# One copy of an expert's first two products for each of four slot counts, chosen at run time by a jump on three engines

## The chip, the cores and the metric

The kernel runs on one core of a Trainium2 chip. The time is the device time of one execution in microseconds (us); lower is better. The core has TensorE (PE in the profile; its weight loads are PEld), VectorE (DVE), ScalarE (ACT), GpSimd (POOL) and SyncE (SP). Each engine works through its own queue of instructions in order and waits on semaphores for the others. DMAs are issued from SP's queue (SPq) and, for the scattered writes, from POOL's.

## The reference: one decoder layer that ends in a mixture of experts

Everything is float32 with 8 x 512 tokens of width 512. The layer is a Mamba block, a cross-attention and a mixture of experts (MoE), each followed by a residual and a LayerNorm. Only the experts matter here:

```python
cap = max(1, int(CAP_FACTOR * N * K / E))            # 640 slots for each of 32 experts
...
pos = (jnp.cumsum(oh, axis=0) * oh).sum(-1) - 1       # place of a token within its expert
keep = pos < cap
...
xe = xp[buf_tok].reshape(E, cap, DIM)                 # unused slots hold zeros
h = jax.nn.silu(jnp.einsum('ecd,edh->ech', xe, w1)) * jnp.einsum('ecd,edh->ech', xe, w3)
out = jnp.einsum('ech,ehd->ecd', h, w2) * buf_w.reshape(E, cap, 1)
y = jnp.zeros((N + 1, DIM), x.dtype).at[buf_tok].add(out.reshape(E * cap, DIM))[:N]
```

A token goes to 4 of 32 experts, so an expert gets 512 tokens on average; every expert has 640 slots, and the slots beyond its tokens are zero rows. With the inputs that the reference sets up, the gate sends these numbers of tokens to experts 0 to 31: 728 555 429 316 439 394 503 606 368 498 370 383 616 500 344 750 553 400 539 555 679 620 480 671 353 536 560 691 680 400 394 474. So 12 experts have at most 448 tokens, 5 have 449 to 512, 6 have 513 to 576 and 9 have more than 576.

## The kernel before: three stages, and the experts one after the other

`layers` (to about 3784 us in the profiled execution) computes the Mamba block, the attention, the gate and the shared expert, and scatters each token's row of 545 numbers (512 features, 32 weights, the token's number) to its slots in a DRAM buffer `xbuf`. `experts` then loops over the 32 experts, and `finish` reads the sums `based` and normalises them.

For each expert `e` the loop does this:

- `load(e + 1)`: SP issues the DMA of the next expert's 640 rows, `xe` (L1250), and then of its weights `w1`, `w3`, `w2` (L1253). The pools hold two of each. So `xe` of expert e+1 goes into the buffer of expert e-1, and must wait until everything that reads that buffer is done. The last readers are the scatters of e-1, which take the token numbers from it.
- `hidden(got, r, side)` for r = 0 and 1: the products of `xe` with `w1` and `w3` by Winograd's form of Strassen's scheme, seven products of quarter size in place of eight. The slots are the moving columns, two halves of 320 (`HALF`). `product` (L1314) is two float32 matmuls, which the trace shows as two records each; seven products for two weights and two r make 112 matmul records for each expert. ACT copies partial sums from PSUM (L1328) and applies SiLU (L1341), DVE adds and multiplies (L1335, L1339) into `hT`.
- `give(e, got, side)`: the product with `w2`, again seven quarter products, 256 columns wide, for the first 512 slots (56 records of `ps_o`), and a plain product `po` (L1416, 8 records) for the last 128 slots. ACT (L1387, L1417, L1444) and DVE (L1391) scale by the token's weight into five tiles `y`. Each is added to `based` by an indirect DMA from POOL (L1394, `put`), first the one of `po`, then the other four. They wait for each other, since all add to the same tensor.
- `side` is work for the next expert that is threaded in: `between` transposes `xe` of e+1 (`flip`: four PE transposes L1285 into one PSUM bank of the pool `e_pst`, one DVE copy L1286) and forms the sums of its slots (`sums_x`, L1293 to L1296) and of its weights (`sums_w` L1276, `sums_w2` L1308).

A scheduler fixes the order on each engine from the program's order, the dependencies and its own idea of times. In its order the transposes of expert e+1 are spread over `give(e)`: one group of four at its start, the other four groups between the products. On DVE the sums for the weights come in `give` and at its end, after the sums of `hT`.

Of the kernel before, what the change touches and what calls it, by code (L numbers as in the profile page):

```python
# [8 lines left out]
F32 = mybir.dt.float32  # L9
I32 = mybir.dt.int32  # L10
# [7 lines left out]
P = 128  # L18
# [21 lines left out]
E = 32  # L40
# [6 lines left out]
SLOTS = E * CAP  # L47
CJ = CAP // P
HALF = CAP // 2

ROW = D + E + 1

# [33 lines left out]
    return wait(roots)  # L86


def layers(ctx, tc, a, x1d, filld, based, xbuf):

# [572 lines left out]
    def locate(any_, pb, pn, st):  # L663
        for j in range(SC):
            nc.vector.tensor_tensor(taken[:, j + 1, :], taken[:, j, :], pn[:, j * E : (j + 1) * E], ALU.add)
        pos = new([E], "g_sc")
        nc.vector.tensor_tensor(
            pos, pb.rearrange("p (j e) -> p j e", j=SC), taken[:, 0:SC, :], ALU.add
        )
        nc.vector.tensor_copy(taken[:, 0, :], taken[:, SC, :])  # L670
        fits = new([E], "g_fits")
        nc.vector.tensor_scalar(fits, pos, float(CAP), None, ALU.is_lt)
        nc.vector.tensor_tensor(pos, pos, first, ALU.add)
        nc.vector.tensor_tensor(pos, pos, fits, ALU.mult)
# [542 lines left out]
    dry()  # L1217


def experts(ctx, tc, a, xbuf, based):  # L1220

# [40 lines left out]
    def B(x, j, k):  # L1262
        return x[:, 2 * j : 2 * j + 2, k * HALF : (k + 1) * HALF]

    def sums_w(got, n):

        w = got[n]
        s1, s2, s4 = (wp.tile([P, 2, FH], F32, tag=f"{n}s{i}", name="s", bufs=1 if n == "hT" else 2) for i in (1, 2, 4))
        got[n, "s"] = s1, s2, A(w, 1, 0), s4
        for o, x, y, op in (  # L1270
            (s1, A(w, 1, 0), A(w, 1, 1), ALU.add),
            (s2, s1, A(w, 0, 0), ALU.subtract),
            (A(w, 1, 0), A(w, 0, 0), A(w, 1, 0), ALU.subtract),
            (s4, A(w, 0, 1), s2, ALU.subtract),
        ):
            nc.vector.tensor_tensor(o, x, y, op)  # L1276
            yield

    def flip(got, j):

        if j == 0:
            got["xT"] = p2.tile([P, DC, CAP], F32, tag="xT", name="xT")
        ps = pst.tile([P, D], F32, tag="tr", name="ps_t")
        for dc in range(DC):
            nc.tensor.transpose(ps[:, dc * P : (dc + 1) * P], got["x"][:, j, dc * P : (dc + 1) * P], ident)  # L1285
        nc.vector.tensor_copy(got["xT"][:, :, j * P : (j + 1) * P], ps.rearrange("p (c t) -> p c t", c=DC))  # L1286

    def sums_x(got):

# [5 lines left out]
        nc.vector.tensor_tensor(B(x, 0, 1), B(x, 1, 1), B(x, 0, 1), ALU.subtract)  # L1295
        nc.vector.tensor_tensor(t4, B(x, 1, 0), t2, ALU.subtract)  # L1296

    def sums_w2(got):

        w = got["w2"]  # L1300
        got["t2"] = t1, t2, t3, t4 = [wp.tile([P, 2, FH], F32, tag=f"w2t{i}", name="t", bufs=1) for i in range(4)]
        for o, x, y in (
            (t1, BW(w, 0, 1), BW(w, 0, 0)),
            (t2, BW(w, 1, 1), t1),
            (t3, BW(w, 1, 1), BW(w, 0, 1)),
            (t4, BW(w, 1, 0), t2),
        ):
            nc.vector.tensor_tensor(o, x, y, ALU.subtract)  # L1308
            yield

    def product(ps, w, r, x, more=False):

        for n in range(2):
            nc.tensor.matmul(  # L1314
                ps, w[:, n, r * P : (r + 1) * P], x[:, n, :], start=not more and n == 0, stop=n == 1,
                skip_group_check=more,
            )

    def hidden(got, r, side):

        x, hT = got["xT"], got["hT"]
        t1, t2, t3, t4 = got["t"]
        ws = [(got[n], *got[n, "s"]) for n in ("w1", "w3")]
        both = range(2)

        def keep(ps, m, tag):
            v = p2.tile([P, HALF], F32, tag=f"{tag}{m}", name=tag)
            nc.scalar.copy(v, ps)  # L1328
            return v

        def use(m, i, k, ps, more=None):
            to = hT[:, 2 * i + r, k * HALF : (k + 1) * HALF]
            if more is not None:
                v = more if m else to
                nc.vector.tensor_tensor(v, ps, more, ALU.add)  # L1335
            else:
                v = ps
            if m:
                nc.vector.tensor_tensor(to, to, v, ALU.mult)  # L1339
            else:  # L1340
                nc.scalar.activation(to, v, AF.Silu)  # L1341

        p1, pu, p5 = [], [], []
        xs = [None, None]
        for m, (w, s1, s2, s3, s4) in enumerate(ws):
            xs[m] = psx.tile([P, HALF], F32, tag="h", name="ps_h")
            product(xs[m], A(w, 0, 0), r, B(x, 0, 0))
            p1.append(keep(xs[m], m, "p1"))
        for m, (w, s1, s2, s3, s4) in enumerate(ws):
            ps = psy.tile([P, HALF], F32, tag="h2", name="ps_h")  # L1350
            product(ps, A(w, 0, 1), r, B(x, 1, 0))
            use(m, 0, 0, ps, p1[m])
        next(side, None)
        for m, (w, s1, s2, s3, s4) in enumerate(ws):
            product(xs[m], s2, r, t2, more=True)
            pu.append(keep(xs[m], m, "pu"))
        next(side, None)
        ys = []
        for m, (w, s1, s2, s3, s4) in enumerate(ws):
            ys.append(psy.tile([P, HALF], F32, tag="h2", name="ps_h"))  # L1360
            product(ys[m], s1, r, t1)
            p5.append(keep(ys[m], m, "p5"))
        next(side, None)
        for m, (w, s1, s2, s3, s4) in enumerate(ws):
            product(xs[m], s3, r, t3, more=True)
            use(m, 1, 1, xs[m], p5[m])
        for m, (w, s1, s2, s3, s4) in enumerate(ws):
            product(ys[m], s4, r, B(x, 1, 1), more=True)
            use(m, 0, 1, ys[m], pu[m])
        next(side, None)  # L1370
        for m, (w, s1, s2, s3, s4) in enumerate(ws):
            product(xs[m], A(w, 1, 1), r, t4, more=True)
            use(m, 1, 0, xs[m])

    def give(e, got, side):

        xe, hT, w2 = got["x"], got["hT"], got["w2"]
        t1, t2, t3, t4 = got["t2"]
# [34 lines left out]
        j = CJ - 1  # L1413
        po = pso.tile([P, D], F32, tag="po", name="po")
        for ic in range(DC):
            nc.tensor.matmul(po, hT[:, ic, j * P : (j + 1) * P], w2[:, ic, :], start=(ic == 0), stop=(ic == DC - 1))  # L1416
        nc.scalar.activation(ys[j], po, AF.Identity, scale=weight(j))  # L1417
        put(j)
        next(side, None)
# [26 lines left out]

    def between(nxt):

        sums = sums_w(nxt, "w3")
        for j in range(CJ):  # L1450
            flip(nxt, j)
# [2 lines left out]
            next(sums, None)  # L1454
            yield

    nxt = load(0)
    for j in range(CJ):
        flip(nxt, j)
    sums_x(nxt)  # L1460
    for n in ("w1", "w3"):
        for _ in sums_w(nxt, n):
# [53 lines left out]

def program(tc, a, out):
    nc = tc.nc
    with tc.tile_pool(name="dram", bufs=1, space=DRAM) as dram:
# [4 lines left out]
        xbuf = dram.tile([SLOTS, ROW], F32, name="xbuf")  # L1524
        nc.scalar.preload_act_table_set(LN_EXP)

        with ExitStack() as ctx:
            layers(ctx, tc, a, x1d, filld, based, xbuf)
        with ExitStack() as ctx:
            experts(ctx, tc, a, xbuf, based)  # L1530
        with ExitStack() as ctx:
            finish(ctx, tc, based, out)

# [30 lines left out]
```

## Time and profile before

| | |
|---|---|
| time, median of 3 runs | 5404.11 us (5396.59 to 5407.47) |
| time of the profiled execution | 5406.28 us |
| its span, first to last instruction | 5404.6 us |
| experts' matmuls, first and last start | 3800.6 and 5333 us |
| one expert, start of its transposes to the next one's | 47.9 us |
| busy over the span | PE 86%, DVE 78%, ACT 48%, POOL 11% |

An engine's line in the profile gives start and duration in us, the source line, the output and inputs, and in brackets how long the engine stood idle before and what ended that. A matmul's duration overlaps the next one's start, so rates are taken from one group's start to the next one's. "Granted clock" (PEclk) is the share of full speed at which TensorE was let run.

### The profile page before, as it was taken

How to read it: one execution, taken by the hardware profiler on the slowest of the kernel's cores; microseconds unless marked ns; L12 is line 12 of the kernel's file. 1: busy time of each engine (PE TensorE's matmuls, PEld its weight loads, DVE VectorE, ACT ScalarE, POOL GpSimd, SP SyncE). 2: the span in 40 equal slices, each digit the busy share in tenths (PEclk: the TensorE clock that was granted, in tenths of full speed). 3: DMA queues.
4: the chain of work that ended last, by engine and by line, in shares of the span. 5: the costliest groups of instructions: out<-in, count | busy, mean ns of one | idle time of the engine just before them, and what ended most of it. 6: DMA issues, size and time to landing. Idle time of an engine off the chain costs nothing. (4 is left out here: it accounts for less than half of the span.)

```text
span 5404.6 us, 53991 instructions
## 1 busy us (share of the span) xinstructions
PE 4672.4 (86%) x17320; PEld 2476.6 (46%) x17320; DVE 4235.9 (78%) x5369; ACT 2593.6 (48%) x5726; POOL 570.3 (11%) x426
## 2 busy tenths in 40 slices
PE   6768889788888988988888888789999999999994
PEld 3324234234333423433333342333677777777773
DVE  7999899989989989898998998943566555665554
ACT  5566565565656556566565655523222222222223
POOL 1000002002000200200200020011111111111111
PEclk8879989999999999999999999899999999999997
DMA  8875346345444634634544463342344444544544
GB/s 236 266 224 146 87 96 208 81 114 176 114 104 117 197 77 109 189 98 107 174 125 100 117 200 78 91 146 66 103 128 127 123 117 118 127 127 121 129 115 144
DMA packets 486427, 719.03 MB, mean 133 GB/s; under 512 B 117137, under 2 KB 200625, under 8 KB 484096
## 3 DMA queue, kind: packets, MB, share of 16 engines
q1 hardware_dynamic: 450128, 627.16, 41.1%
q0 software_dynamic: 33280, 76.90, 7.5%
q10 hardware_dynamic: 2736, 11.54, 0.5%
q8 instruction: 137, 2.24, 0.2%
q14 instruction: 146, 1.20, 0.1%
HBM read 391.24 MB, written 165.05 MB: 103 GB/s over the span
## 5 line engine op out<-in xcount | busy, mean ns | idle before, releaser
L480 ACT ACTIVATE l_da<-rep,l_aneg 128x256 f32<-128x256 f32 x2048 | 895.0, 501 | 941.8 <-DVE h L501 877.0
L501 DVE TENSOR_TENSOR_SCAN h<-l_da,h 128x1028 f32<-128x1028 f32 x512 | 1166.0, 2292 | 20.3 <-ACT l_da L480 17.7
L494 DVE TENSOR_TENSOR h<-rep,bc 128x1024 f32<-128x1024 f32 x512 | 614.7, 1218 | 103.1 <-PE py L521 84.6
L510 DVE TENSOR_TENSOR h<-h,bc 128x1024 f32<-128x1024 f32 x512 | 619.5, 1217 | 2.1
L521 PE MATMUL py<-h,l_fold 128*32 128x512 f32 x2048 | 368.3, 644 | 113.4 <-DVE h L510 96.5
L813 PE MATMUL ps_s<-l_ka,l_qa 64*128 64x512 f32 x1024 | 325.6, 707 | 137.8 <-DVE mx L815 137.6
L1314 PE MATMUL ps_h<-xT,w 128*128 128x320 f32 x1536 | 435.8, 433 | 0.0
L1394 POOL DMA_INDIRECT based<-y,xe x160 | 255.5, 1597 | 1309.9 <-ACT y L1417 630.0
L1335 DVE TENSOR_TENSOR hT<-ps_h,p 128x320 f32<-128x320 f32 x128 | 62.9, 492 | 378.5 <-PE ps_h L1314 378.5
L815 DVE TENSOR_REDUCE mx<-ps_s 128x2 f32<-128x1024 f32 x256 | 310.2, 1217 | 58.5 <-PE ps_s L813 58.3
L1314 PEld LDWEIGHTS ps_h<-xT,w 128*128 128x128 f32 x1536 | 292.5, 191 | 118.3 <-issue 0.4
L855 PE MATMUL po<-eT,l_va 128*64 128x512 f32 x1024 | 301.5, 670 | 47.6 <-ACT eT L843 43.1
L839 PE MATMUL ps_t<-l_qa,l_ka 64*128 64x512 f32 x1024 | 308.4, 674 | 23.8 <-ACT eT L843 23.1
L843 ACT ACTIVATE eT<-ps_t 128x1024 f32<-128x1024 f32 x256 | 259.0, 1015 | 128.8 <-PE ps_t L839 128.5
L688 POOL DMA_INDIRECT xbuf<-x2t,dest x128 | 217.2, 1697 | 860.4 <-DVE dest L679 760.8
L1314 PE MATMUL ps_h<-t,s 128*128 128x320 f32 x1024 | 286.1, 432 | 0.0
L343 PE MATMUL ps_z<-xnT,wm 128*128 128x256 f32 x1024 | 238.0, 388 | 30.0 <-DVE o L561 24.3
L750 PE MATMUL ps_p<-x2T,wa 128*128 128x512 f32 x512 | 241.5, 626 | 18.1 <-ACT hT L944 10.4
L552 PE MATMUL po<-wm,zs 128*128 128x512 f32 x512 | 244.7, 632 | 13.8 <-DVE z L957 11.9
L343 PE MATMUL ps_x<-xnT,wm 128*128 128x256 f32 x1024 | 246.5, 393 | 4.5 <-ACT xnT L332 2.5
L343 PEld LDWEIGHTS ps_z<-xnT,wm 128*128 128x128 f32 x1024 | 194.6, 193 | 93.0 <-DVE o L561 37.5
L343 PEld LDWEIGHTS ps_x<-xnT,wm 128*128 128x128 f32 x1024 | 196.1, 195 | 80.5 <-issue 43.8
(232 smaller groups left out, 7170.4 us busy)
## 6 DMA issues: line engine op xcount, KB each, us to landing
w<-in_w SPq DMA_DIRECT2D x93, 1024.0 KB
wm<-in_in_proj_w SPq DMA_DIRECT2D x128, 512.0 KB
rep<-dt SPq DMA_DIRECT2D x256, 256.0 KB
rep<-dtx SPq DMA_DIRECT2D x256, 256.0 KB
xbuf<-zero SPq DMA_DIRECT2D x32, 1362.5 KB
xe<-xbuf SPq DMA_DIRECT2D x32, 1362.5 KB
wm<-in_out_proj_w SPq DMA_DIRECT2D x64, 512.0 KB
wa<-in_sw SPq DMA_DIRECT2D x24, 1024.0 KB
```

The costliest lines, as they stand in the source:

```text
L343: nc.tensor.matmul(ps[:, i, :], w[:, dc, i * P : (i + 1) * P], f["xnT"][:, dc, :], start=(dc == 0), stop=(dc == DC - 1),)
L480: nc.scalar.activation(da[:, n, 1:], dt[:, j, i, :], AF.Exp, scale=aneg[:, 2 * q + i, 2 * jj + j, g : g + 1])
L494: nc.vector.tensor_tensor(h[:, :, 1:], dtx.rearrange("p j i t -> p (j i) t"), f["bc", g][0], ALU.mult)
L501: nc.vector.tensor_tensor_scan(flat, da.rearrange("p n t -> p (n t)"), flat, 0.0, ALU.mult, ALU.add)
L510: nc.vector.tensor_tensor(h[:, :, 0:T], h[:, :, 1:], f["bc", g][1], ALU.mult)
L521: nc.tensor.matmul(f["py"][j * QP : (j + 1) * QP, :, :], fold, hs[j // 2][:, 2 * (j % 2) : 2 * (j % 2) + 2, 0:T], start=False, stop=g == N ...
L813: nc.tensor.matmul(ps[:, j, :], qa[r, lt * P : (lt + 1) * P], ka[r, :], start=True, stop=True)
L815: return lambda: nc.vector.tensor_reduce(mx[:, lt, :].unsqueeze(2), ps, AX.X, ALU.max) and None
L839: nc.tensor.matmul(ps[:, j, :], ka[r, kc * P : (kc + 1) * P], qa[r, :], start=True, stop=True)
L843: nc.scalar.activation(eT, ps, AF.Exp)
L855: nc.tensor.matmul(po[j * 2 * HD : (j + 1) * 2 * HD, :], va[:, kc, i, j * HD : (j + 2) * HD], eT[:, j, :], start=(kc == 0), stop=(kc == SC ...
L1314: nc.tensor.matmul(ps, w[:, n, r * P : (r + 1) * P], x[:, n, :], start=not more and n == 0, stop=n == 1, skip_group_check=more,)
```

## The change

The last image's gate in `layers` also writes, for every expert, a number from 0 to 3 into a small tile `arm`: how many of 448, 512 and 576 its token count exceeds. The slots of an expert are dealt to the two halves in turn (even slots to the first, odd to the second), so that the first 2c slots are the first c columns of both halves. The two calls of `hidden` are written out four times, for c = 224, 256, 288 and 320 columns (`COLS`), and PE, ACT and DVE each jump to one copy by the number in `arm`. The slots beyond 2c are set to zero in `hT`. During `give(e)` each of the three engines loads the number for e+1 into a register and gives a hint for the coming jump (`announce`); each copy ends in a jump to the common code behind it. The PSUM pool of the transposes gets a second bank, that of `po` loses one. `give`, its columns and the scatters are as before. Buffers are allocated (`room_w`, `room_w2`) ahead of the jump, since the copies share them.

```diff
+COLS = tuple(range(224, HALF + 1, 32))
...
+        if not clock:
+            many = taken[:, SC, :]
+            more = taken[:, 1, :]
+            nc.vector.tensor_scalar(more, many, float(2 * COLS[0]), None, ALU.is_gt)
+            for c in COLS[1:-1]:
+                to = arm if c == COLS[-2] else more
+                nc.vector.scalar_tensor_tensor(to, many, float(2 * c), more, ALU.is_gt, ALU.add)
...
-    pst = ctx.enter_context(tc.tile_pool(name="e_pst", bufs=1, space=PSUM))
-    pso = ctx.enter_context(tc.tile_pool(name="e_pso", bufs=2, space=PSUM))
+    pst = ctx.enter_context(tc.tile_pool(name="e_pst", bufs=2, space=PSUM))
+    pso = ctx.enter_context(tc.tile_pool(name="e_pso", bufs=1, space=PSUM))
...
-        nc.vector.tensor_copy(got["xT"][:, :, j * P : (j + 1) * P], ps.rearrange("p (c t) -> p c t", c=DC))
+        to = got["xT"].rearrange("p c (k t) -> p c k t", k=2)[:, :, :, j * P // 2 : (j + 1) * P // 2]
+        nc.vector.tensor_copy(to, ps.rearrange("p (c t k) -> p c k t", c=DC, k=2))
...
+        cols = ps.shape[-1]
         for n in range(2):
             nc.tensor.matmul(
-                ps, w[:, n, r * P : (r + 1) * P], x[:, n, :], start=not more and n == 0, stop=n == 1,
+                ps, w[:, n, r * P : (r + 1) * P], x[:, n, 0:cols], start=not more and n == 0, stop=n == 1,
...
         def use(m, i, k, ps, more=None):
-            to = hT[:, 2 * i + r, k * HALF : (k + 1) * HALF]
+            to = hT.rearrange("p c (t k) -> p c t k", k=2)[:, 2 * i + r, 0:cols, k]
...
-            nc.scalar.activation(v, ps, AF.Identity, scale=weight(j))
+            ins = nc.scalar.activation(v, ps, AF.Identity, scale=weight(j))
+            if tag == "p1" and r and e + 1 < E:
+                announce(which, e + 1, ins)
...
-        for _ in sums_w(got, "hT"):
+        room_w(got, "hT")
+        for ins in sums_w(got, "hT"):
             pass
+        if e + 1 < E:
+            announce(which, e + 1, ins)
...
+            ins = nc.tensor.matmul(
+                po, hT[:, ic, j * P : (j + 1) * P], w2[:, ic, :], start=(ic == 0), stop=(ic == DC - 1)
+            )
+        if e + 1 < E:
+            announce(which, e + 1, ins)
...
+    def choice(k, e):
+        return engines[k].value_load(arm[0:1, e : e + 1])
+
+    def announce(which, e, ins):
+        k = ins.ins.engine
+        with tc.issue_after(ins.ins):
+            which[k] = choice(k, e)
+            tc.switch_hint({k: which[k]}, len(COLS), label=f"cols{e}")
...
+    which = {k: choice(k, 0) for k in engines}
     for e in range(E):
         got, nxt = nxt, load(e + 1) if e + 1 < E else None
         got["hT"] = p2.tile([P, DC, CAP], F32, tag="hT", name="hT", bufs=1)
-        for r in range(2):
-            hidden(got, r, sums_w2(got) if r == 0 else sums_w(nxt, "w1") if nxt else iter(()))
-        give(e, got, between(nxt) if nxt else iter(()))
+        room_w2(got)
+        if nxt:
+            room_w(nxt, "w1")
+        for n in tc.Switch(which, len(COLS), hint=f"cols{e}" if e else None):
+            if COLS[n] < HALF:
+                nc.vector.memset(got["hT"][:, :, 2 * COLS[n] :], 0.0)
+            for r in range(2):
+                side = sums_w2(got) if r == 0 else sums_w(nxt, "w1") if nxt else iter(())
+                hidden(got, r, side, COLS[n])
+        give(e, got, between(nxt) if nxt else iter(()), which)
```

The scheduler can't mix what is inside the copies with what is outside, so the order around them changes too. In the built program, `layers` is as before but for the three small DVE operations. In an expert's `give`, PE now does one matmul of `po` and then all five groups of transposes in a row, the remaining matmuls of `po` among the first products, and then the products as before. DVE does the five copies, `sums_x`, and only then the sums of `hT`, its register load and hint, and the scaling of `y` with the sums of `w3` between. Each copy begins on DVE with the fill of `hT` (not for 320), which waits for the end of `give` on PE, and all eight sums of `w2` and of the next `w1`, ahead of the first addition for `hT`. SP and POOL take no part in the choice; SP's load of `xe` waits for the same five scatters as before.

More of the change, by code (lines that the diff above doesn't have):

```diff
@@ L86, in layernorm, with layers @@
     return wait(roots)
-def layers(ctx, tc, a, x1d, filld, based, xbuf):
+def layers(ctx, tc, a, x1d, filld, based, xbuf, arm):
     nc = tc.nc
@@ L1217, in layers, with experts @@
     dry()
-def experts(ctx, tc, a, xbuf, based):
+def experts(ctx, tc, a, xbuf, based, arm):
     nc = tc.nc
@@ L1263, in B, with room_w @@
         return x[:, 2 * j : 2 * j + 2, k * HALF : (k + 1) * HALF]
+    def room_w(got, n):
+        s1, s2, s4 = (wp.tile([P, 2, FH], F32, tag=f"{n}s{i}", name="s", bufs=1 if n == "hT" else 2) for i in (1, 2, 4))
+        got[n, "s"] = s1, s2, A(got[n], 1, 0), s4
     def sums_w(got, n):
         w = got[n]
-        s1, s2, s4 = (wp.tile([P, 2, FH], F32, tag=f"{n}s{i}", name="s", bufs=1 if n == "hT" else 2) for i in (1, 2, 4))
-        got[n, "s"] = s1, s2, A(w, 1, 0), s4
+        s1, s2, _, s4 = got[n, "s"]
         for o, x, y, op in (
@@ L1275, in sums_w @@
         ):
-            nc.vector.tensor_tensor(o, x, y, op)
-            yield
+            yield nc.vector.tensor_tensor(o, x, y, op)
     def flip(got, j):
@@ L1296, in sums_x, with room_w2 @@
         nc.vector.tensor_tensor(t4, B(x, 1, 0), t2, ALU.subtract)
+    def room_w2(got):
+        got["t2"] = [wp.tile([P, 2, FH], F32, tag=f"w2t{i}", name="t", bufs=1) for i in range(4)]
     def sums_w2(got):
         w = got["w2"]
-        got["t2"] = t1, t2, t3, t4 = [wp.tile([P, 2, FH], F32, tag=f"w2t{i}", name="t", bufs=1) for i in range(4)]
+        t1, t2, t3, t4 = got["t2"]
         for o, x, y in (
@@ L1311, in product, with hidden @@
     def product(ps, w, r, x, more=False):
+        cols = ps.shape[-1]
         for n in range(2):
             nc.tensor.matmul(
-                ps, w[:, n, r * P : (r + 1) * P], x[:, n, :], start=not more and n == 0, stop=n == 1,
+                ps, w[:, n, r * P : (r + 1) * P], x[:, n, 0:cols], start=not more and n == 0, stop=n == 1,
                 skip_group_check=more,
             )
-    def hidden(got, r, side):
+    def hidden(got, r, side, cols):
         x, hT = got["xT"], got["hT"]
@@ L1326, in keep @@
         def keep(ps, m, tag):
-            v = p2.tile([P, HALF], F32, tag=f"{tag}{m}", name=tag)
+            v = p2.tile([P, HALF], F32, tag=f"{tag}{m}", name=tag)[:, 0:cols]
             nc.scalar.copy(v, ps)
@@ L1345, in hidden @@
         for m, (w, s1, s2, s3, s4) in enumerate(ws):
-            xs[m] = psx.tile([P, HALF], F32, tag="h", name="ps_h")
+            xs[m] = psx.tile([P, HALF], F32, tag="h", name="ps_h")[:, 0:cols]
             product(xs[m], A(w, 0, 0), r, B(x, 0, 0))
@@ L1349, in hidden @@
         for m, (w, s1, s2, s3, s4) in enumerate(ws):
-            ps = psy.tile([P, HALF], F32, tag="h2", name="ps_h")
+            ps = psy.tile([P, HALF], F32, tag="h2", name="ps_h")[:, 0:cols]
             product(ps, A(w, 0, 1), r, B(x, 1, 0))
@@ L1359, in hidden @@
         for m, (w, s1, s2, s3, s4) in enumerate(ws):
-            ys.append(psy.tile([P, HALF], F32, tag="h2", name="ps_h"))
+            ys.append(psy.tile([P, HALF], F32, tag="h2", name="ps_h")[:, 0:cols])
             product(ys[m], s1, r, t1)
@@ L1373, in hidden, with give @@
             use(m, 1, 0, xs[m])
-    def give(e, got, side):
+    def give(e, got, side, which):
         xe, hT, w2 = got["x"], got["hT"], got["w2"]
@@ L1415, in give @@
         for ic in range(DC):
-            nc.tensor.matmul(po, hT[:, ic, j * P : (j + 1) * P], w2[:, ic, :], start=(ic == 0), stop=(ic == DC - 1))
+            ins = nc.tensor.matmul(
[3 more added lines that the diff above has]
+            announce(which, e + 1, ins)
         nc.scalar.activation(ys[j], po, AF.Identity, scale=weight(j))
@@ L1447, in between @@
     def between(nxt):
+        room_w(nxt, "w3")
         sums = sums_w(nxt, "w3")
@@ L1455, in between @@
             yield
+    engines = {mybir.EngineType.PE: nc.tensor, mybir.EngineType.Activation: nc.scalar, mybir.EngineType.DVE: nc.vector}
+    def choice(k, e):
[5 more added lines that the diff above has]
+            tc.switch_hint({k: which[k]}, len(COLS), label=f"cols{e}")
     nxt = load(0)
@@ L1461, in experts @@
     for n in ("w1", "w3"):
+        room_w(nxt, n)
         for _ in sums_w(nxt, n):
             pass
+    which = {k: choice(k, 0) for k in engines}
     for e in range(E):
@@ L1518, in program @@
     nc = tc.nc
-    with tc.tile_pool(name="dram", bufs=1, space=DRAM) as dram:
+    with tc.tile_pool(name="dram", bufs=1, space=DRAM) as dram, tc.tile_pool(name="one", bufs=1) as one:
         x1d = dram.tile([N, D], F32, name="x1d")
@@ L1524, in program @@
         xbuf = dram.tile([SLOTS, ROW], F32, name="xbuf")
+        arm = one.tile([P, E], I32, name="arm")
         nc.scalar.preload_act_table_set(LN_EXP)
         with ExitStack() as ctx:
-            layers(ctx, tc, a, x1d, filld, based, xbuf)
+            layers(ctx, tc, a, x1d, filld, based, xbuf, arm)
         with ExitStack() as ctx:
-            experts(ctx, tc, a, xbuf, based)
+            experts(ctx, tc, a, xbuf, based, arm)
         with ExitStack() as ctx:
```

## The prediction

> **What bounds the kernel now.** I read the engines by window first. In the experts' stage PE never rests and runs at full clock, with DVE 58% busy:
>
> ```profile
> 4000.00:4500.00 500.00, 499.64 (x2037) 368.15 (x2036) 289.10 (x522) 139.66 (x305) 84.59 (x53) 1.00 0.49 121
> ```
>
> The columns are the window, its length, busy us of PE, PEld, DVE, ACT and POOL, the granted clock, the DMA share and GB/s. Then the timeline of PE for one expert, at the seam of `hidden` and `give`:
>
> ```profile
> 4499.86 2.32 PE L1314 MATMUL ps_h<-xT,s 128*128 128x320 f32 x8
> 4502.01 2.32 PE L1314 MATMUL ps_h<-t,w 128*128 128x320 f32 x8
> 4504.16 0.60 PE L1285 MATMUL ps_t<-e_ident,xe 128*128 128x128 f32 x4
> 4504.60 1.89 PE L1314 MATMUL ps_o<-w,hT 128*128 128x256 f32 x8
> 4506.33 3.60 PE L1416 MATMUL po<-w,hT 128*128 128x512 f32 x8
> ```
>
> Eight records of 320 columns take 2.15 us start to start (0.269 each), eight of 256 take 1.73 (0.216), so a column costs 0.83 ns. Four transposes take 0.44, `po` 3.43. An expert is 112 x 0.269 = 30.15 us of `hidden` and 17.7 us of `give`: 47.86, and the next one's transposes indeed start at 4552.0.
>
> But a second chain runs almost as long. POOL's scatters and SP's load of `xe`, by timeline:
>
> ```profile
> 4520.16 1.54 POOL L1394 DMA_INDIRECT based<-y,xe  x1 [7.49 <-DVE y L1391]
> 4527.77 1.54 POOL L1394 DMA_INDIRECT based<-y,xe  x1 [6.07 <-DVE hT L1339]
> 4533.32 1.54 POOL L1394 DMA_INDIRECT based<-y,xe  x1 [4.01 <-ACT hT L1341]
> 4538.85 1.54 POOL L1394 DMA_INDIRECT based<-y,xe  x1 [3.98 <-ACT p L1328]
> ```
>
> ```profile
> 4543.50 0.37 SPq L1250 DMA_DIRECT2D xe<-xbuf  x1
> ```
>
> and the windows behind that load (last column GB/s):
>
> ```profile
> 4545.50:4547.50 2.00, 2.00 (x9) 1.38 (x8) 0.49 (x1) 0.49 (x2) 0.00 (x0) 1.00 1.01 373
> 4547.50:4549.60 2.10, 2.10 (x9) 1.47 (x8) 1.40 (x3) 0.49 (x2) 0.00 (x0) 1.00 0.68 263
> 4549.60:4551.10 1.50, 1.50 (x7) 1.10 (x6) 0.92 (x2) 0.39 (x1) 0.00 (x0) 1.00 0.00 0
> ```
>
> The scatter of `y0` is issued 16.0 us after the transposes start, the four scatters take 23.3 us, the load lands 6.1 us later (4549.6). PE wants it at 4552.0: **2.4 us of slack in 47.9**. The queue's waits confirm the cause:
>
> ```profile
> SPq L1250 <- DMA based<-y,xe: 673.9, 69, 24.0
> ```
>
> **The change, part by part** (against the profiled execution's own 5406.3 us).
>
> 1. *Fewer columns.* From the token counts: 320 columns for 9 experts, 288 for 6, 256 for 5, 224 for 12. `hidden` falls from 30.15 to 112 x (0.242, 0.216, 0.189) = 27.2, 24.2, 21.2 us. If PE's work were all, that is 6 x 3.0 + 5 x 6.0 + 12 x 9.0 = 156 us. Weight loads don't stop it at 224: the transposes load a weight each every 0.11 us.
>
> 2. *Transposes in a row.* Each group of four now waits for the copy of the group two before. The copy's row:
>
> ```profile
> L1286 DVE COPY xT<-ps_t 128x512 f32<-128x512 f32 x157 | 107.8, 687 | 7.5 <-PE ps_t L1285 7.5
> ```
>
> A copy starts 0.24 us after its transposes (4504.60 to 4504.84), the copies follow each other at 0.60, and the next group starts 0.06 after a copy's end (seen ahead of expert 0: 3796.02 to 3796.08). That puts the groups at 0, 0.44, 1.43, 2.03, 2.86 and the end at 3.30 instead of 2.2: **+1.1 us** on PE for each expert. DVE then does `sums_x` (4 x 0.75 to 0.85) and the sums of `hT`, whose second ends about 8.8 us after the transposes' start; PE asks for it at 3.30 + 0.86 + 1.73 + 1.72 + 1.73 = 9.3, so this costs nothing.
>
> 3. *Sums ahead of the first addition.* In a copy DVE waits for PE (0.25), fills (768 to 256 elements; DVE's rows of 320 and 640 take 0.49 and 0.82, about 1 ns an element, so at most 0.8 to 0.27) and does eight sums at 0.61; the first addition is done about 6.2, 6.05, 5.95 us after `give` ends for 224, 256, 288. PE needs it after 24 records, 4.5, 5.2, 5.8 us: **+1.7, +0.9, +0.15**. For 320 (no fill, no wait) nothing.
>
> 4. *The jumps.* PE's sequencer meets them with 1.7 us of matmuls queued (the last eight records of `give` or of `hidden`, whose waits were met earlier); DVE has 1.2 us before PE lets it fill, and ACT some 2 us of slack before PE needs its first copy. The register loads lie behind 1.7 us of `po` on PE and 1.2 us of sums on DVE. The trace has no jump or load. Lower end 0; upper end 4 us per expert, two missed fetches of code on PE: the page has code arriving in pieces,
>
> ```profile
> q8 instruction: 137, 2.24, 0.2%
> ```
>
> 16.4 KB each, about the 14 KB of one copy (224 instructions at the 64 bytes that 2.24 + 1.20 MB of code for 53,991 instructions give); 0.2% of 16 engines' span is 1.3 us a piece, and a load takes about 2 us from issue to first bytes (4503.28 to 4505). I take 0.2, nearer the lower end, since the hint comes 10 us ahead. [...]
>
> 5. *The chain of scatters.* It is not shortened. After the change `y0` is scattered 3.30 + 0.86 + 1.73 + 1.72 + 1.73 + 3 x 1.73 + 0.86 + 1.0 = 16.4 us after the transposes start, and the next `xe` lands 23.3 + 6.1 us later: no expert can take less than **45.8 us**. PE alone would need 0.86 (the first matmul of `po`) + 18.0 + `hidden` + part 3: 49.0 for 320, 46.2 for 288, 44.0 for 256, 41.8 for 224. So 320 gains -1.1, 288 gains 1.65, and 256 and 224 both gain only 2.06, while PE waits 1.8 and 4.0 us for `xe`.
>
> 6. *The clock.* Such a wait slows TensorE afterwards. Two windows of 3.4 us, of layers' part:
>
> ```profile
> 1025.70:1029.10 3.40, 1.69 (x8) 0.47 (x8) 3.30 (x4) 3.40 (x8) 0.00 (x0) 1.00 0.01 2
> 1029.10:1032.50 3.40, 3.40 (x8) 0.48 (x8) 3.40 (x3) 3.32 (x9) 0.00 (x0) 0.50 0.19 58
> ```
>
> Half busy, then a window at half clock. Counted in steps of 3.41 us over the span, all 86 full-clock windows under 45% busy were followed by one at half; that is 1.9 us of idling. A half window loses at most 1.7 us of work, right where `y0` is due, so the floor of part 5 moves with it. A wait of 4.0 always triggers it; averaged over where it falls it costs about 1.6, less 0.6 since slow transposes no longer wait for copies: 1.0 x 12. A wait of 1.8 triggers it half the time: 0.75 x 4. Together 15; bounds 0 and 38 (16 x 2.4, some staying slow for two windows). [...]
>
> 7. *Ends.* Three operations for `arm`: 3 x 0.17. Expert 0: four more groups of transposes, an unannounced jump and part 3's sums, less the groups that leave its `give`: +2 (0 to 6). Expert 31 (256) has no transposes after it: 6.0 - 0.9 = -5.1.
>
> **The sum**, for experts 1 to 31: 8 x 1.14 - 6 x 1.65 - 16 x 2.06 + 15 + 14 x 0.2 + 2 - 5.1 + 0.5 = -18.6, so 5387.7 us, or 5385.5 from the median, which the profiled run exceeds by 2.2. I say **5387**.
>
> **The rivals.**
>
> - *The chain doesn't hold PE* (scatters turn out quicker): then 224 and 256 gain 6.1 and 3.9 and no clock is lost: 9.1 - 9.9 - 12 x 6.1 - 4 x 3.9 + 0.2 = -89, 5317. Against it: the 2.4 us of slack and the same five waits in front of `xe`. 0.05.
> - *The clock eats the gain*: every wait for `xe` costs 2.4 us. 16 x 2.4 in place of 15 gives 5411, no change within what can be told. For it: the windows above; against it: waits of 4 us leave mostly one slow window. 0.18.
> - *The jumps cost PE code fetches* (slower): two misses of 3.3 us, each covered by 1.7, cost 3.2 us for the 14 experts of 320 and 288, and 1.4 for the four of 256, where the wait for `xe` absorbs the rest: 51 in place of 3, 5436. It decides from 1.5 us per expert on. For it: 14 KB skipped at each jump; against it: the hint. 0.20.
> - *All experts take the widest copy* (a wrong number in `arm`): 31 x 1.34 + 2.5 = 44 more, 5450. Nothing in the arithmetic of the counts speaks for it. 0.05.
>
> **How the numbers follow.** The forecast has 0.52; with floors 1 us lower or higher and the clock's bounds it spans 5354 to 5405, and I put 0.42 of it below 5393. About 0.2% (11 us) can be told from no change. Faster: 0.42 + 0.05 = 0.47. Same: 0.10 + 0.14 + 0.02 = 0.26. Slower: 0.04 + 0.18 + 0.05 = 0.27. The range reaches from the forecast's low end to the third rival: 5352 to 5438.
>
> **What would show it.** After: records of 224 to 320 columns by these counts; PE idle in front of the transposes until `xe` lands for 224 and 256; an expert's step of 46 to 47.5 us for these and 49 for 320; half-clock windows in a stage that had none; idle PE at the first matmul of a copy would show the third rival. Steps near 42 us would prove part 5 wrong.

## The result: slower by 2.3%

The changed kernel takes 5528.47 us (median of 4 runs, 5521.15 to 5538.59) beside 5405.79 us for the kernel before on the same chip: ratio 1.0231, 95% interval 1.0211 to 1.0252. The forecast was 5387 us, its range ended at 5438. From expert 0's `po` to expert 31's, 31 steps of the loop, the profile of before shows 1484.9 us and that of after 1600.4; this span of 31 steps is the yardstick below, since it leaves out what the layers ahead do. (The profiled execution of the changed kernel is the slowest of its four.)

### The profile page after: what moved, and what is told of

It reads as the page before. It is cut to its first block, busy times and chain, and to the rows that moved or that the text cites. A ratio compares the mean times of both kernels' runs of the same rounds, so it can differ in the third digit from the quotient of the medians.

```text
span 5536.8 us, 55268 instructions
## 1 busy us (share of the span) xinstructions
PE 4598.4 (83%) x17320; PEld 2513.6 (45%) x17320; DVE 4212.6 (76%) x5395; ACT 2562.1 (46%) x5726; POOL 577.0 (10%) x426
## 5 line engine op out<-in xcount | busy, mean ns | idle before, releaser
L1330 PE MATMUL ps_h<-xT,w 128*128 128x224 f32 (+3 forms) x1536 | 370.8, 391 | 5.6 <-issue 5.6
L1330 PE MATMUL ps_h<-t,s 128*128 128x224 f32 (+3 forms) x1024 | 259.6, 405 | 49.3 <-ACT p L1344 41.5
L1351 DVE TENSOR_TENSOR hT<-ps_h,p 128x224 f32<-128x224 f32 (+3 forms) x128 | 55.8, 436 | 274.1 <-PE ps_h L1330 267.6
L1298 DVE COPY xT<-ps_t 128x512 f32<-128x512 f32 x160 | 107.6, 689 | 202.5 <-PE ps_t L1296 156.3
L1296 PE MATMUL ps_t<-e_ident,xe 128*128 128x128 f32 x640 | 127.3, 360 | 154.5 <-DMA xe<-xbuf 107.1
```

The lines of the kernel that those rows point to most:

```text
L1330: nc.tensor.matmul(ps, w[:, n, r * P : (r + 1) * P], x[:, n, 0:cols], start=not more and n == 0, stop=n == 1, skip_group_check=more,)
```

## The profile after

The window of the experts' stage first (same columns as in the prediction):

```profile
4000.00:4500.00 500.00, 433.00 (x1916) 357.29 (x1915) 270.61 (x509) 118.22 (x283) 80.10 (x49) 0.93 0.46 114
```

PE, which never rested, is now idle 67 of 500 us, and its clock, 1.00 before, is 0.93. So the path no longer runs through PE alone. The seam of `hidden` and `give` of expert 7, which has 320 columns, on PE's timeline:

```profile
4204.82 2.32 PE L1330 MATMUL ps_h<-t,w 128*128 128x320 f32 x8
4206.97 1.02 PE L1437 MATMUL po<-w,hT 128*128 128x512 f32 x2
4207.83 1.04 PE L1296 MATMUL ps_t<-e_ident,xe 128*128 128x128 f32 x8
4209.22 1.25 PE L1296 MATMUL ps_t<-e_ident,xe 128*128 128x128 f32 x8 [0.35 <-DVE xT L1298]
4210.66 0.66 PE L1296 MATMUL ps_t<-e_ident,xe 128*128 128x128 f32 x4 [0.19 <-DVE xT L1298]
4211.15 1.02 PE L1437 MATMUL po<-w,hT 128*128 128x512 f32 x2
```

The transposes run in a row and end 3.32 us after they start (3.30 forecast). The scatters and the load of `xe` behind them:

```profile
4224.18 1.54 POOL L1412 DMA_INDIRECT based<-y,xe  x1 [5.61 <-DVE y L1409]
4233.14 1.54 POOL L1412 DMA_INDIRECT based<-y,xe  x1 [7.42 <-DVE hT L1355]
4238.59 1.54 POOL L1412 DMA_INDIRECT based<-y,xe  x1 [3.91 <-ACT p L1344]
4244.15 1.54 POOL L1412 DMA_INDIRECT based<-y,xe  x1 [4.02 <-ACT p L1344]
```

```profile
4250.25 0.37 SPq L1258 DMA_DIRECT2D xe<-xbuf  x1
```

and PE at the head of the next `give`, behind a copy of 224 columns:

```profile
4247.70 1.02 PE L1437 MATMUL po<-w,hT 128*128 128x512 f32 x2
4257.01 3.20 PE L1296 MATMUL ps_t<-e_ident,xe 128*128 128x128 f32 x13 [8.29 <-DMA xe<-xbuf]
```

`y0` goes out 16.35 us after the transposes' start (16.4 forecast), but PE waits 8.3 us for `xe`, where 4.0 was reckoned. Expert 7 is of the kind that kept the forecast: over the whole stage the same distance is 16.4 to 16.6 us behind copies for 320 columns, 17.3 to 18.5 behind those for 224, and 19.2 to 23.1 behind those for 256 and 288. Two more lines, from the timelines of DVE and ACT, had no counterpart before. DVE at the end of a copy for 256 columns:

```profile
4304.48 0.42 DVE L1355 TENSOR_TENSOR hT<-hT,ps_h 128x256 f32<-128x256 f32 x1 [0.84 <-PE ps_h L1330]
4310.24 1.29 DVE L1298 COPY xT<-ps_t 128x512 f32<-128x512 f32 x2 [5.33 <-issue]
```

and ACT at the entry of one:

```profile
4276.35 0.47 ACT L1469 ACTIVATE y<-ps_o,xe 128x256 f32<-128x256 f32 x1 [0.39 <-PE ps_o L1330]
4282.71 0.65 ACT L1344 COPY p<-ps_h 128x256 f32<-128x256 f32 x2 [5.89 <-issue]
```

"issue" is time in which the engine waited for nothing that the profile shows. Each of these gaps holds a jump. The trace also records the branches themselves. On DVE and ACT a branch is 0.04 to 0.05 us long and the wait comes behind it, so the table gives the time from the branch's end to the next instruction of its engine. On PE the wait lies inside the branch's own record, and at an entry the next instruction follows at most 0.13 us later; so for PE the table gives the branch's length. Experts 1 to 31, in us:

| | into 224 (first copy) | into 256, 288, 320 | out of 224 | out of 256, 288 | out of 320 (last copy) |
|---|---|---|---|---|---|
| PE, the branch itself | 0.3 to 0.6 (one 3.4) | 0.3 to 0.4 (one 3.1) | 0.3 | 0.3 | 0.3 |
| DVE | 0.4 to 0.5 | 4.1 to 5.1 (14 of 19; four 0.5, one 2.7) | hidden behind the wait for `xe` | 5.2 to 5.8 (one 2.9) | 1.2, a wait for PE included |
| ACT | 0.3 to 0.4 | 4.2 to 6.3 (18 of 19) | 2.5 to 3.8 | 2.5 to 4.6 | 0.4 |

PE, with its hints, jumps almost for nothing: behind its two long branches it stands 0.9 and 1.0 us, and nowhere else. ACT and DVE mostly pay 2.5 to 6 us, but for the jumps into the first copy and out of the last. What PE itself waits for between 3900 and 5400 us (tile, line, what it waited for: sum, times, longest):

```profile
PE ps_t L1296 <- DMA xe<-xbuf: 90.5, 14, 8.7
PE ps_t L1296 <- DVE xT L1298: 46.3, 27, 4.8
PE ps_h L1330 <- ACT p L1344: 36.6, 16, 3.4
```

The first is the wait for `xe`, the second falls mostly behind the exits and the third behind the entries. The page has the code that arrives:

```profile
q8 instruction: 207, 3.39, 0.3%
q14 instruction: 336, 2.75, 0.2%
```

before, q8 brought 137 pieces and q14 146. That is 260 more pieces for 31 passes through the loop. That the gaps are waits for code is inferred from these pieces and from what the hint does below; the trace doesn't name what an engine waits for there.

## The experiments

**Theory:** the jumps hold ACT and DVE for code, these hold PE, and what they delay lengthens the chain from `y0`'s scatter to the next `xe`. **Rival 1:** the new order (transposes in a row, sums ahead) is the cost. **Rival 2:** the chain of scatters is long by itself once PE no longer hides it. All ratios are against the kernel before, run on the same chip, with 95% intervals.

| run | median us | ratio | 31 steps, us |
|---|---|---|---|
| before | 5405.79 | 1 | 1484.9 |
| after | 5528.47 | 1.0231 (1.0211 to 1.0252) | 1600.4 |
| static_cols | 5382.15 | 0.9954 (0.9938 to 0.9971) | 1465.6 |
| static_320 | 5398.52 | 0.9987 (0.9978 to 0.9997) | 1483.8 |
| row_320 | 5428.26 | 1.0048 (1.0029 to 1.0067) | 1514.2 |
| jump_320 | 5518.96 | 1.0214 (1.0197 to 1.0231) | 1598.0 |
| jump_first | 5639.54 | 1.0441 (1.0413 to 1.0468) | 1722.8 |
| no_hint | 5568.00 | 1.0306 (1.0280 to 1.0331) | 1641.2 |
| two_copies | 5485.51 | 1.0158 (1.0137 to 1.0178) | 1569.7 |
| after_xe3 | 5494.68 | 1.0168 (1.0151 to 1.0185) | 1565.1 |
| before_xe3 | 5404.76 | 0.9997 (0.9986 to 1.0008) | 1485.1 |
| static_xe3 | 5310.97 | 0.9822 (0.9798 to 0.9847) | 1394.8 |
| late_flips | 5460.87 | 1.0105 (1.0086 to 1.0124) | 1538.4 |
| late_flips_xe3 | 5460.41 | 1.0108 (1.0083 to 1.0134) | 1546.0 |
| late_sums | 5395.19 | 0.9978 (0.9968 to 0.9988) | 1470.6 |
| late_sums_xe3 | 5344.68 | 0.9889 (0.9872 to 0.9905) | 1420.7 |
| static_sums_xe3 | 5241.69 | 0.9696 (0.9680 to 0.9712) | 1328.6 |

### Without jumps: static_cols and static_320

```diff
+TAKE = (3, 2, 0, 0, 0, 0, 1, 3, ...)      # (3,) * 32 in static_320
-        for n in tc.Switch(which, len(COLS), hint=f"cols{e}" if e else None):
+        for n in (TAKE[e],):
```

> The changed kernel without jumps, hints and loads of the expert's number: each expert's column count is fixed when the program is built, from the token counts of these inputs, so that the arithmetic, its order and its buffers are those of the changed kernel in a straight line. Theory (the jumps make ACT and DVE fetch code late, and what they delay holds PE and the next load of xe): 5365 to 5395 us, steps of 46 to 49 us per expert, no ACT copy of L1344 that starts 3 us or more late, transposes done in 3.3 us wherever xe is there. Rival 1 (the new order, transposes in a row and sums ahead, is the cost): 5480 to 5530. Rival 2 (the chain of scatters and the load of xe is long by itself, now that PE no longer hides it): 5440 to 5480, with waits for xe behind each narrow expert as long as in the changed kernel.

> As static_cols, but all 32 experts at 320 columns: only the order, the layout of the slots and the PSUM shares of the change are left, no jump and no narrower product. Theory (jumps): 5410 to 5440, the 1.1 us per expert that the prediction gave the transposes in a row. Rival 1 (new order): 5490 to 5540. Rival 2 (chain): 5410 to 5440 as well, since at 320 columns PE still hides the chain.

Without the jumps the same columns take 5382.15 us, 146 us less than the changed kernel, as the theory had it. At 320 columns everywhere it is 5398.52, below the theory's range and a little below the kernel before (its experts begin 5.4 us earlier, its 31 steps are about the same). It isn't a clean stroke against rival 1, though. Without the jump the scheduler again spreads the transposes over `give`, as before the change; so the order that the changed kernel runs belongs to the jump, and row_320 below had to test it by itself. And rival 2 has its share: the narrower products save only 16.4 us in static_cols (5398.52 to 5382.15), a tenth of what PE saves. The one wait that PE has left in static_cols, between 3900 and 5300 us:

```profile
PE ps_t L1297 <- DMA xe<-xbuf: 103.2, 21, 7.9
```

The waits for DVE's copies and for ACT that the changed kernel has are gone; the wait for `xe` is not. An expert of 224 columns behind another one takes some 47.6 us there, not the 38.9 that PE's own work comes to.

### All jumps, one width: jump_320

```diff
-            nc.vector.tensor_scalar(more, many, float(2 * COLS[0]), None, ALU.is_gt)
+            nc.vector.tensor_scalar(more, many, -1.0, None, ALU.is_gt)
-                nc.vector.scalar_tensor_tensor(to, many, float(2 * c), more, ALU.is_gt, ALU.add)
+                nc.vector.scalar_tensor_tensor(to, many, -1.0, more, ALU.is_gt, ALU.add)
```

> The changed kernel with both thresholds replaced so that every expert's number is 3: all jumps, hints and loads stay, and each expert takes the copy for 320 columns, the last of the four. Theory (jumps): 60 to 120 us above static_320, so 5480 to 5550, with ACT's first copies of L1344 late by 3 to 6 us in most experts, but the transposes in 3.3 us everywhere, because this copy ends beside the common code. Rivals 1 and 2: within 15 us of static_320.

120 us above static_320: the top of the theory's range. The timelines of ACT and PE at one entry:

```profile
4259.69 0.47 ACT L1469 ACTIVATE y<-ps_o,xe 128x256 f32<-128x256 f32 x1 [0.39 <-PE ps_o L1330]
4265.52 0.75 ACT L1344 COPY p<-ps_h 128x320 f32<-128x320 f32 x2 [5.36 <-issue]
```

```profile
4259.49 4.47 PE L1330 MATMUL ps_h<-xT,w 128*128 128x320 f32 x16
4266.00 4.57 PE L1330 MATMUL ps_h<-t,s 128*128 128x320 f32 x16 [2.04 <-ACT p L1344]
```

ACT can't jump before it has taken in the last product of `give`; then it is 5.4 us late, and PE, which has 16 records to do without it (4.3 us), stands 2 us. DVE comes 4.3 us late at the same place, and nobody waits for it. At the exit all gaps are short, and the transposes take 3.3 us everywhere.

### The other end: jump_first

```diff
-COLS = tuple(range(224, HALF + 1, 32))
+COLS = (HALF,) * 4
-            nc.vector.tensor_scalar(more, many, float(2 * COLS[0]), None, ALU.is_gt)
+            nc.vector.tensor_scalar(more, many, 1e6, None, ALU.is_gt)
```

> The changed kernel with four copies that are all 320 columns wide, of which every expert takes the first; jumps, hints and loads stay. Theory (a jump costs by how far it goes): the entry is short on all three engines (0.1 to 0.5 us) and the exit past three copies long, about 2.8 us on DVE and 2.5 to 3.5 on ACT as behind the 224-column copies of the changed kernel; the transposes then take 4 to 6 us in place of 3.2 and y0's scatter comes later: 5470 to 5530. Rival (the order alone, with nothing for the jump): 5430 to 5445.

The mechanism is as expected: every entry is short (PE 0.1, DVE 0.4 to 0.5, ACT 0.4) and every exit long. The price was not: 5639.54 us, 110 above my range. I had read 2.8 us for DVE's exit off the 224-column copies; here it is 5.1 to 5.7 but for the last two experts, and PE's first work behind the exit needs DVE at once:

```profile
4321.73 1.04 PE L1295 MATMUL ps_t<-e_ident,xe 128*128 128x128 f32 x8
4328.27 0.69 PE L1295 MATMUL ps_t<-e_ident,xe 128*128 128x128 f32 x2 [5.51 <-DVE xT L1297]
```

So a late exit costs 6.7 us per expert ((1722.8 - 1514.2) / 31, against row_320), a late entry 2.7 ((1598.0 - 1514.2) / 31). As row_320 is not quite the changed kernel's order (see below), the same against static_320 with 1.13 us per expert added for the order: 6.6 and 2.6.

### Two copies

```diff
-COLS = tuple(range(224, HALF + 1, 32))
+COLS = (256, HALF)
```

(`arm` then needs one comparison in place of three.)

> The changed kernel with two copies in place of four: 256 columns (17 experts) and 320 (15). Theory (in the runs so far an entry is short only into the first copy and an exit only out of the last, so a middle copy pays twice): now each expert pays one of the two, 17 pay an exit of some 5 us on DVE and 15 an entry of some 5 us on ACT and 4 on DVE: 5475 to 5515 us, below the changed kernel though its products save less (101 us of PE in place of 155). Rival (the number of copies doesn't matter, each jump costs the same): 5530 to 5570.

5485.51 us: the theory. The branches show it expert by expert: into the copy for 256 columns 0.4 to 0.5 us on DVE and, but for two, 0.4 on ACT, out of it 5.2 to 7.4 on DVE in all but two; into the copy for 320 mostly 4 to 6 on both, out of it 1.2 and 0.4.

### Without hints

```diff
-            tc.switch_hint({k: which[k]}, len(COLS), label=f"cols{e}")
...
-        for n in tc.Switch(which, len(COLS), hint=f"cols{e}" if e else None):
+        for n in tc.Switch(which, len(COLS)):
```

> The changed kernel without the hints ahead of the jumps; the loads of the expert's number stay where they are. Theory (in the changed kernel's trace the instruction after the jump starts 0.1 us after it on PE and mostly 4 to 6 us after it on DVE and ACT, so the hint buys nothing there): 5515 to 5545 us, the same three gaps. Rival (the hint is what keeps PE at 0.1 us and makes some of the short gaps on DVE and ACT): PE then pays some 3 to 5 us per expert, 5600 to 5680.

By its time neither. 40 us above the changed kernel: the hint ahead of the entry is worth 1.3 us per expert. In kind the rival is right for PE: its branch into any copy but the first is now 3.3 to 4.0 us long, in all 19 cases, and 0.3 to 0.4 into the first. Its queued products cover about half of that; then it stands 1.3 to 2.0 us at the copy's first product, 32 us in all. Between 3900 and 5250 us:

```profile
PE ps_h L1330 <- issue: 27.5, 16, 2.0
```

The changed kernel has two such waits, of 0.9 and 1.0 us. DVE's long entries take 6.0 to 7.6 us in place of 4.1 to 5.1, ACT's stay at 5.2 to 6.4. So the hint covers nearly all of PE's wait (0.3 to 0.6 us with it) and a third of DVE's; on ACT no run shows an effect. The trace has a second hint on each of the three engines, the first instruction of each copy (L1509), 20 us or more ahead of the exit. It stays in no_hint, and DVE's and ACT's exits are long all the same; what it is worth no run shows.

### The order alone: row_320

static_320 with the changed kernel's order put on it by hand:

```diff
+        with tc.issue_after(last["sum"].ins) if e + 1 < E else ExitStack():
             for ins in sums_w(got, "hT"):
...
+            with tc.issue_after(last["flip"].ins) if e + 1 < E else ExitStack():
                 product(xs[r], A(hT, 0, 0), r, BW(w2, 0, 0))
```

(all five transposes are written ahead of these lines; `last` holds the last transpose and the last sum of `xT`.)

> static_320 with the order of the changed kernel put on it by hand: PE issues the transposes of the next expert in a row at the head of the second half instead of one by one between the products, and DVE adds up xT before it adds up hT; no jump, 320 columns everywhere. Theory (what the prediction gave this order, 1.1 us per expert, is right): 5425 to 5445. Rival 1 (the order costs as much as the jumps): over 5480. Rival 2 (the order is free): within 8 us of static_320.

29.7 us above static_320, 0.98 us per expert, inside the theory's range. But that it comes so near to the 1.1 us of the prediction is luck, since it is not made of the same waits. With no jump the scheduler put matmuls of `po` between the groups of transposes and drew products of the next `hidden` forward into `give`; PE waits for no copy there. It waits 16.5 us in all for DVE's `y` in `give` and 3.7 us for `xe`. In jump_320, which has the changed kernel's order, the seam can be read directly: from the end of `hidden` to the next copy 18.85 us, in static_320 17.72, so 1.13 us, 35 us for 31 experts. The other part of the order, the sums ahead, costs PE 7.7 us in the changed kernel. So rival 1 is some 43 us, under a third of the 146.

### The third buffer for xe

```diff
-        got["x"] = xe = p2.tile([P, CJ, ROW], F32, tag="xe", name="xe")
+        got["x"] = xe = p2.tile([P, CJ, ROW], F32, tag="xe", name="xe", bufs=3)
```

> The changed kernel with three buffers for xe in place of two: the load of xe no longer waits for the scatters of the expert before. Theory (jumps): the late ACT and DVE still hold PE, but the wait for xe goes: 5400 to 5450. Rival 2 (chain by itself): 5300 to 5360, since nothing else is late. Rival 1 (new order): 5490 to 5530, no wait for xe being the cause.

> The kernel before with three buffers for xe. At 320 columns PE hides the chain with 2.4 us to spare, so both theories say no change: 5395 to 5415. If it were faster, the gain of static_xe3 would not belong to the narrower products.

> static_cols with three buffers for xe. Theory (without jumps, what is left of the loss is the chain of scatters and the load of xe behind them): PE becomes the bound, the 155 us of narrower products (9, 6, 5, 12 experts by 0, 2.95, 5.95 and 8.95 us) all show against static_320: 5240 to 5290. Rival (something else is as long as the chain, the weights' buffers or POOL's scatters): 5330 to 5375.

before_xe3 shows no change, as all expected. The other two gain, 34 and 71 us, but both less than I had said: after_xe3 misses the theory's 5450 by 45 us (it falls into rival 1's range, but row_320 leaves that rival no more than 30 us), static_xe3 misses 5290 by 21. Something else was late.

### Work behind the exit that needs no DVE: late_flips

The five transposes are queued on PE behind `po`:

```diff
+        with tc.issue_after(ins.ins):          # the last matmul of po
+            for _ in side:
+                pass
```

> The changed kernel with the transposes of the next expert queued behind the product of the last 128 tokens (po), so that PE has some 7 us of products to do while DVE comes out of its copy. Theory (the exit costs because PE's first work behind it needs DVE at once): the 5 us behind the 256- and 288-column copies go (11 experts), and y0's scatter comes earlier, so the wait for xe shrinks as well: 5400 to 5460 us. Rival (PE waits for DVE later all the same, or xe sets the pace): 5500 to 5530.

> late_flips with three buffers for xe. Theory: with exit and xe covered what is left is the entry, where ACT's first copy is late by some 5 us and holds PE 2 to 4 us in the 20 experts that don't take the first copy: 5330 to 5400 us, below the kernel before. Rival: as after_xe3, 5480 to 5500.

late_flips gains 68 us against the changed kernel, 0.9 us short of what I had said; the third buffer on top gives nothing: 5460.41 us, above the theory's 5400 and below the rival's 5480. The timelines of late_flips_xe3 behind a narrow copy (DVE, PE, SP's queue) name the next wait:

```profile
4224.65 1.29 DVE L1298 COPY xT<-ps_t 128x512 f32<-128x512 f32 x2
4233.54 0.69 DVE L1288 TENSOR_TENSOR s<-w 128x512 f32<-128x512 f32 x1 [7.60 <-DMA w<-in_w]
```

```profile
4226.76 1.03 PE L1330 MATMUL ps_o<-w,hT 128*128 128x256 f32 x4
4234.89 1.11 PE L1296 MATMUL ps_t<-e_ident,xe 128*128 128x128 f32 x4 [7.10 <-DVE xT L1298]
```

```profile
4219.56 0.37 SPq L1258 DMA_DIRECT2D xe<-xbuf  x1
4220.02 1.72 SPq L1261 DMA_DIRECT2D w<-in_w  x2
```

DVE stands 7.6 us at its first sum over `w3`, with three copies of the transposes queued behind it. That sum starts 0.3 us after the last packet of the weights issued at 4220: they were loaded behind `xe` in SP's queue, which waits for the scatters. The scheduler had put the sums over `w3` an expert early (they read the weights of expert e+2 during `give(e)`), in the changed kernel, in the one before and in the static ones alike; at 47.9 us a step nothing waited for it.

### The sums where they are needed: late_sums

```diff
+        t4 = sums_x(nxt)
+        with tc.issue_after(t4.ins):
+            for _ in sums:
+                pass
```

(static_sums_xe3 has these lines too, and the sums over `w1` queued behind the last multiplication of the first `hidden` call.)

> late_flips with DVE's sums over w3 queued behind its sums over xT, so that they read the weights of the next expert and not those of the one after it. Theory (these early sums wait for weights that are loaded just in time, with the copies of the transposes queued behind them): the 4 to 5 us behind narrow copies go, but with two buffers the wait for xe takes their place in part: 5420 to 5455 us. Rival (they hide nothing else): 5455 to 5470.

> late_sums with three buffers for xe. Theory (the wait for weights ate what the third buffer gave): 12 experts at 224 columns near 40 us, the others 46 to 52 because of ACT's late entry: 5340 to 5400 us, below the kernel before. Rival (the jumps alone ate the gain): 5440 to 5470, as late_flips_xe3.

> static_xe3 with DVE's sums over w1 and w3 queued so that none runs an expert early; no jumps, column counts fixed when the program is built. Theory: the waits for weights (96 us on DVE in static_xe3) go and PE is the bound: 5240 to 5285 us, static_320 less the 155 us of narrower products. Rival (another wait of the same length stands behind them): 5300 to 5315.

late_sums falls by 66 us, further than I had said; with the third buffer it reaches 5344.68 us, and without jumps 5241.69, both inside their ranges. In static_sums_xe3 PE is the bound again, at full clock:

```profile
4000.00:4500.00 500.00, 500.00 (x2306) 415.31 (x2305) 324.41 (x613) 146.11 (x343) 92.98 (x59) 1.00 0.55 139
```

and its 31 steps are 155.2 us shorter than static_320's, the whole of the narrower products. late_sums_xe3 is the version that beats both kernels and still reads the counts at run time: ratio 0.9889 (0.9872 to 0.9905). An expert of 224 columns takes 39.9 us there. The exit is still as late as before, but PE now has work (DVE, then PE):

```profile
4085.18 0.42 DVE L1355 TENSOR_TENSOR hT<-hT,ps_h 128x256 f32<-128x256 f32 x1 [0.84 <-PE ps_h L1330]
4090.31 0.69 DVE L1288 TENSOR_TENSOR s<-hT 128x512 f32<-128x512 f32 x1 [4.71 <-issue]
```

```profile
4084.91 1.88 PE L1436 MATMUL po<-w,hT 128*128 128x512 f32 x4
4086.63 1.89 PE L1330 MATMUL ps_o<-w,hT 128*128 128x256 f32 x8
4088.36 1.88 PE L1436 MATMUL po<-w,hT 128*128 128x512 f32 x4
4090.07 1.04 PE L1296 MATMUL ps_t<-e_ident,xe 128*128 128x128 f32 x8
4090.95 0.60 PE L1330 MATMUL ps_o<-w,hT 128*128 128x256 f32 x2
4093.59 0.66 PE L1296 MATMUL ps_t<-e_ident,xe 128*128 128x128 f32 x4 [2.05 <-DVE xT L1298]
```

DVE stands 4.7 us on "issue"; PE feels 2.05 of it. The 92 us by which its 31 steps exceed those of static_sums_xe3 are what the jumps and the order around them still cost, some 3 us per expert.

## Why the prediction was wrong, point by point

The step that failed is part 4, **"I take 0.2, nearer the lower end, since the hint comes 10 us ahead"**. Against static_cols, the jumps and the order that comes with them cost 146 us by the medians and 135 by the 31 steps, 4.3 to 4.7 us per expert; with 1.1 to 1.4 of it for the order, some 3 to 3.6 are the jumps'. That lies inside the bounds of 0 and 4 that I had set, and I chose the wrong end. PE shows where it went: 46.3 us of waits mostly behind the exits and 36.6 behind the entries, which static_cols hasn't, and half clock for 174 us of the stage in place of 99. Three things were wrong in the choice:

- *The engine.* I bounded two missed fetches on PE. With the hint PE's branch is long at two of 31 entries (3.1 and 3.4 us) and at none of the exits (0.3 us); what I trusted the hint to do, it does there. ACT waits 2.5 to 6.3 us at 41 of its 62 jumps and DVE 2.7 to 5.8 at 26 (12 more are hidden by the wait for `xe`), and that I didn't price.
- *The cover.* I gave DVE 1.2 us and ACT 2 us at the entry and thought that enough. In jump_320 ACT loses 5.0 us (5.4 in place of 0.4) and PE stands 2.0 of them, so the cover is 3 us and the gap longer; DVE's 4.3 us hold nobody there. And I looked at entries only: I named no cover for the exit, where the new order puts transposes that need DVE first. jump_first prices that at 6.7 us per expert, more than twice the entry's 2.7.
- *The hint.* It is real, 40 us by no_hint, nearly all of PE's wait, but it takes only a third off DVE's entry, and on ACT's no run shows an effect (5.2 to 6.4 us without it, 4.2 to 6.3 with it). It leaves a pattern that I had not reckoned with: short into the first copy (0.3 to 0.6 us on all three engines, but for one 3.4 on PE) and out of the last (0.3 on PE, 0.4 on ACT, 1.2 on DVE with a wait for PE), mostly long otherwise on ACT and DVE. Without it PE is not spared either, as its 3.3 to 4.0 us in no_hint show.

The third rival had the kind of loss and the threshold (from 1.5 us per expert on), but on PE and at a third of the size: 5436. Its price, 3.3 us a miss with 1.7 covered, is what no_hint shows for PE's entry, 3.3 to 4.0 with 1.3 to 2.0 left over.

The other terms:

- *Part 1* is right: 155.2 us measured where PE is the bound, 155 by the counts (6 x 2.99 + 5 x 5.97 + 12 x 8.96).
- *Part 2* is right: 1.13 us at the seam, 1.1 forecast.
- *Part 3* is too large: PE's waits for DVE's first additions are 0.29 us at the entry of expert 8 (224 columns) and 7.7 us in the whole stage; I had 1.7 x 12 and 0.9 x 5, some 25 us. In the copy for 224 columns six of the eight sums run ahead of the first addition, not all eight as the section on the change and my sum have it.
- *Part 5* is right in kind and short in size. `xe` holds PE in static_cols; the step of narrow experts is some 47.6 us, the floor was to be 45.8. Most of the 1.8 us between is part 6: behind a wait PE runs at half clock where `y0` is due (in static_cols the eight products behind the wait that ends at 4016 us take 3.2 us, those from 4024 on 1.7), and `y0` goes out 17.6 to 18.3 us after the transposes' start in place of 16.0. In the changed kernel the late exits delay `y0` by up to 7 us more (the figures beside the seam above). The link from `y0`'s scatter to the next is longer there as well, 9.2 us on average where before had 7.3 and row_320 has 7.6; jump_320 shows 9.1, so it comes with the jumps. In both kernels 1 MB of weights moves in that time; in the changed one some 50 KB of code do so too, where before had 6. The weights' last packet lands 6.8 us after `y0`'s scatter is issued (before 4.9), the scatter's own 8.1 us (before 6.2). That the code holds up the weights and these the scatter is the likely way, but no run takes it apart. Each expert's one branch on POOL and on SP, which the section on the change doesn't mention, isn't it: `y0`'s scatter starts 0.28 us after DVE's product nearly everywhere, before and after.
- *Part 6* is right in kind and too small: from 3850 us on static_cols spends 169.5 us at half clock, 70.5 of them behind the last expert's products; the kernel before spends 69.8, all of them there.
- *Part 7* wasn't told apart.

That static_cols (5382) lies near my sum without its jump term (5385) is partly chance: it has not the order of parts 2 and 3, and pays more for parts 5 and 6.

What the prediction did not see at all is how the waits stand in line: behind the exit `xe`, behind `xe` the weights, which the scheduler reads an expert early. Removing one showed the next (68, 66 and 50 us), and only all three together gave the gain of the narrower products a way out.

## What to carry to other kernels

Price a jump on every engine that takes it, at both ends, and ask at each end what the engine's first instruction there is and who needs it; put work in front that doesn't need the late engine. When a shorter product is to pay, look up what was just in time at the old pace (a buffer, a load, a sum that a scheduler put early): each of these becomes the bound in turn. Undoing the control flow while keeping the arithmetic (static_cols) tells within one run which half of such a change is at fault, once it is known what order of work went away with it.

## What the runs showed of the hardware that I had not expected

- A branch shows its wait in two ways. On PE it lies inside the branch's own record: 0.3 to 0.6 us with a hint 12 us ahead (29 of 31 entries of the changed kernel), 3.3 to 4.0 us without it into any copy but the first. On ACT and DVE the record is 0.05 us long and the gap follows it. ACT, whose copies have 31 instructions where PE's have some 225, paid 4.2 to 6.3 us into all but the first copy (18 of 19).
- Distance doesn't set ACT's price. At the prediction's 64 bytes per instruction a copy of 31 instructions is 2 KB, so if the copies lie one behind the other the farthest begins some 6 KB behind the first (an estimate); yet ACT took 4.2 to 6.0 us into the second copy (one 0.4) and 5.1 to 5.8 into the fourth.
- Where the code lies seems to count. In jump_320, where every expert takes the same copy, DVE's entry is short (0.5 us) at experts 3, 8, 13, 18, 23 and 28, every fifth, and ACT's (0.4 us) at 11 and 22, every eleventh. PE's two long branches are at experts 25 and 29 in after, jump_320 and jump_first alike. What it is about the place no run shows.
- The wait behind a branch is longer than a piece of code takes to arrive: in jump_320, between ACT's branch at 4259.9 us and its next instruction at 4265.4, three 8 KB pieces of code arrive (at 4260.85, 4263.81 and 4264.70), each in 0.3 us; the trace doesn't say for which engine.
- A hint 7 us ahead shortened DVE's entry from about 6.1 to 4.4 us and left ACT's at 5.5 us, with the hint 11.6 us ahead of the branch.
- Exits differ with no cause that the runs show: DVE's out of the first copy takes 5.1 to 5.7 us in jump_first (the last two experts 3.0 and 2.7) and 2.7 to 3.7 in late_flips.
